# A graph network in four layers on one core: the projection of layer 0's second convolution in seven block products, with other buffers, fetches and start

## The chip, the cores and the metric

One core of one Trainium2 chip runs the whole program, in one launch. The metric is the device time in microseconds (us), the median of several runs. All arithmetic is fp32.

## The reference, cut to what matters

The input is 128 graphs of 64 nodes with 256 features, and one adjacency matrix of 64x64 for all. Four layers follow one another; each normalizes the features, takes the positive part, computes an update and adds it. The change is in layer 0, which is a graph convolution done twice and then four LSTMs over windows of 1, 2, 3 and 4 consecutive nodes, each of which writes its last hidden state back:

```python
h = jax.nn.relu(jnp.einsum('ts,bsh->bth', adj, x @ Wg0 + bg0))
h = jax.nn.relu(jnp.einsum('ts,bsh->bth', adj, h @ Wg1 + bg1))
for p in range(1, MAX_SKIP + 1):
    ...
    last = _lstm_last(Wih[p - 1], Whh[p - 1], bih[p - 1], bhh[p - 1], wins)
    h = h.at[:, idx, :].set(last.reshape(Bv, nw, Hd))
```

Here b is the graph and t the node. Layer 1 is a spectral convolution with attention and an MLP, layer 2 attention over a graph, layer 3 a transform with the eigenvectors of the graph's Laplacian; all of them use the same 64x64 matrix.

## The kernel before, in words

The 8192 tokens stand as 64 tiles of 128 tokens (two graphs each). Layer 0 works on 8 groups of 8 tiles (`NG`, `GT`), a group in two halves of 4 tiles (`HT`). Its results go to DRAM (`put`), and layers 1 to 3 work on 16 groups of 4 tiles, each of which runs through all three layers.

`layer0` (line 1411) does one group: fetch the tokens (two DMAs of 512 KB), norm statistics (`ln_stats`, line 1289: two DVE instructions a tile, four on POOL for the group of tiles), positive part on ACT, product with the adjacency (`mix`, line 1259, a burst of 64x64 matmuls), product with `Wg[0]`, a second mix into `ayT`, and then, feature-major, the projection with `Wg[1]` into `hT`. That projection makes, for each half and each of the two blocks of 128 output rows, two accumulated products of 128x128 by 128x512; its evacuation is a DVE maximum with the bias and a POOL addition. Then the LSTM steps follow: the first step of each window by `lstm_step` (line 1309), the later ones by `lstm_fast` (line 1359). `lstm_fast` computes a 2x2 block product in 7 block products instead of 8: sums of the weight blocks are made once (`fastw`, line 1165, on POOL), sums of the data blocks by `pieces` (line 1343), and partial results are passed on by ACT copies and DVE additions between two PSUM buffers, one of kind "bank" and one of kind "seed". At the end of a group the tokens are fetched a second time, to be added.

The order of all instructions is made ahead by `Plan` (lines 61 to 350): every operation is recorded with an engine and a cost, `schedule` (line 232) runs through the time of a model of the engines and puts the ready operation of the best rank next, and `issue` (line 343) emits them in that order. So every engine's queue has a fixed order, and in the profile every instruction has line 349; tiles tell them apart. What sets the order:

- `rank` (line 333): older groups first; a `lead` makes an operation count as of an older or younger group. The eigen-decomposition of the 64x64 matrix (`spectrum`, line 1193; group `EIG`) runs beside layer 0 on DVE with the lowest rank, on PE and POOL with the highest. Its work space, the arena, serves as big buffers once it is done.
- `window` (line 1052): how many groups may be under way; one more for fetches on SP.
- Pools of buffers (line 904): `big` (128x1024), `mid` (128x512), `stat`, `attn`, 6 PSUM banks and 2 seeds. A value takes a free buffer when its first operation is placed; `reserve` (line 1055) keeps some for the oldest group. After layer 0, `more(mids, ...)` (line 1050) turns the middle buffers into big ones.
- `plan.behind`: an operation that is recorded while it is set waits for the one it names.
- `burst` (line 105): what is recorded inside is one indivisible operation of the plan.

At the start (lines 1097 to 1160) ACT's queue fetches group 0's tokens in five pieces, SP's queue the weights; 14 products of a matrix of ones come first on PE; then row sums of the adjacency are made (`pb`, line 1146: one product with ones, one with the column `rscol`) and the bias tables C0T and B1T from them. Group 0 does its front two tiles at a time.

Of the kernel before, what the change touches and what calls it, by code (L numbers as in the profile page):

```python
# [8 lines left out]
ALU = mybir.AluOpType  # L9
# [3 lines left out]
N = 64  # L13
# [55 lines left out]
class Plan:  # L69
# [111 lines left out]
    def cost(op, aps):  # L181
# [7 lines left out]
        if op.name == "dma_start" and op.eng != "SP":  # L189
            return 0.6, 4.0  # L190
# [713 lines left out]
NBIG, NMID, NSTAT, NATTN = 14, 10, 14, 4  # L904
# [108 lines left out]
def gnn_kernel(ctx: ExitStack, tc: tile.TileContext, a, out):  # L1013
# [38 lines left out]
    def window(oldest):  # L1052
        return max(oldest, 0) + 3 - oldest if oldest < NG - 1 else REST + 4 - oldest if oldest < REST else 8
# [92 lines left out]
    pb = bank("rs")  # L1146
    PE.matmul(pb[:, :N], ones[:N], adjT2[:N], start=True, stop=True)
    PE.matmul(pb[:, N:2 * N], rscol[:N].to_broadcast([N, P]), adjT2[:N], start=True, stop=True)
    rsrow = C([P, 2, 2, N], "rsrow")
    V.tensor_copy(rsrow, pb[:, :2 * N].rearrange("p (r n) -> p r n", r=2).unsqueeze(2).to_broadcast([P, 2, 2, N]))  # L1150


    V.tensor_scalar(nB0, nB0, rscol, -1.0, op0=ALU.mult, op1=ALU.mult)
    C0T = C([P, 2, P], "C0T")
    B1T = C([P, 2, 2, P], "B1T")
    row = lambda r: rsrow[:, r].rearrange("p r n -> p (r n)")
    for c in range(2):
        V.tensor_scalar(C0T[:, c], row(1), bgc[0][:, c:c + 1], None, op0=ALU.mult)
        for t in range(2):
            V.tensor_scalar(B1T[:, t, c, :], row(0), bgc[1][:, c:c + 1], 1.0 if t else -1.0, op0=ALU.mult, op1=ALU.mult)  # L1160
# [128 lines left out]
    def ln_stats(src, n=HT):  # L1289
# [8 lines left out]
        G.tensor_scalar(rs[:, 0, :], mv[:, :, 1], 1e-5, None, op0=ALU.add)  # L1298
        G.tensor_tensor(rs[:, 0, :], rs[:, 0, :], mhalf[:, :n], op=ALU.pow)
        G.tensor_tensor(rs[:, 1, :], mv[:, :, 0], rs[:, 0, :], op=ALU.mult)  # L1300
        G.tensor_scalar(rs[:, 1, :], rs[:, 1, :], -1.0, None, op0=ALU.mult)
# [108 lines left out]

    def layer0(fetched):
        x = fetched()
        plan.lead = 1
# [3 lines left out]
        for t0 in range(0, GT, nl):  # L1417
# [7 lines left out]
            ps = mix(lambda t, c: h[t // 2][:, t % 2, tok(c)], lambda t: adjTb, nl)  # L1425
            for j in range(0, nl, 2):
# [17 lines left out]
        for hf in range(2):  # L1444
            ts = slice(hf * GT // 2, (hf + 1) * GT // 2)
            for m in range(2):
# [3 lines left out]
                dst = hT[m].rearrange("p (n t) -> p n t", t=GT)[:, :, ts]  # L1450
                b1 = [B1T[:, i, m, :].unsqueeze(2).to_broadcast([P, P, GT // 2]) for i in range(2)]
                V.tensor_tensor(dst, ps.rearrange("p (t n) -> p n t", n=P), b1[0], op=ALU.max)
                G.tensor_tensor(dst, dst, b1[1], op=ALU.add)
# [367 lines left out]
```

## Time and profile before

| | |
|---|---|
| time, median of 3 runs | 2100.99 us (2100.03 to 2101.82) |
| profiled execution: time, span | 2099.95 us, 2098.2 us |
| mean granted TensorE clock | 0.998 |
| PE, DVE, ACT, POOL busy | 2065.2, 1767.8, 1097.0, 777.8 us |
| layer 0's groups stored | from 232 us (group 0) to 1340 us (group 7) |
| first product of layer 1 | 1283.7 us |
| last write of the eigenvectors, their first use in layer 3 | 1227.8 us, 1473.4 us |

In the profile PE is TensorE's matmul, PEld its weight load, DVE VectorE, ACT ScalarE, POOL GpSimd, SP the queue that issues DMAs. A line of a group of instructions has the engine, the operation, what is written and read, the shapes and the count; then the busy time in us and the mean of one in ns; then the engine's idle time just before them. Each fp32 product shows as two matmul records. A line of a stretch has its ends, its length, and for each engine the busy time and, in brackets, the number of instructions; the last three numbers are the granted TensorE clock, the DMA engines' busy share and GB/s.

### The profile page before, as it was taken

How to read it: one execution, taken by the hardware profiler on the slowest of the kernel's cores; microseconds unless marked ns; L12 is line 12 of the kernel's file. 1: busy time of each engine (PE TensorE's matmuls, PEld its weight loads, DVE VectorE, ACT ScalarE, POOL GpSimd, SP SyncE). 2: the span in 40 equal slices, each digit the busy share in tenths (PEclk: the TensorE clock that was granted, in tenths of full speed). 3: DMA queues.
4: the chain of work that ended last, by engine and by line, in shares of the span. 5: the costliest groups of instructions: out<-in, count | busy, mean ns of one | idle time of the engine just before them, and what ended most of it. 6: DMA issues, size and time to landing. Idle time of an engine off the chain costs nothing.

```text
span 2098.2 us, 48166 instructions
## 1 busy us (share of the span) xinstructions
PE 2065.2 (98%) x17928; PEld 1678.8 (80%) x17928; DVE 1767.8 (84%) x6691; ACT 1097.0 (52%) x2465; POOL 777.8 (37%) x1162
## 2 busy tenths in 40 slices
PE   8999999999999999999999999999999999999998
PEld 6689689689779778878878789987887788788776
DVE  7799899899999999999988954877878878885787
ACT  3344544544443453444444435575667666664674
POOL 7422221221211122022010123677557576854354
PEclk9999999999999999999999999999999999999999
DMA  6000100100100100000000211200100100000001
GB/s 231 1 3 3 63 2 2 62 2 2 61 1 1 61 2 1 21 26 2 30 12 1 98 44 33 82 2 1 42 22 1 35 29 22 12 12 11 2 1 62
DMA packets 44875, 57.84 MB, mean 28 GB/s; under 512 B 8928, under 2 KB 38496, under 8 KB 44640
## 3 DMA queue, kind: packets, MB, share of 16 engines
q1 hardware_dynamic: 43536, 53.71, 8.0%
q8 instruction: 141, 2.31, 0.5%
q10 hardware_dynamic: 1104, 1.05, 0.2%
q14 instruction: 94, 0.77, 0.1%
HBM read 37.53 MB, written 16.78 MB: 26 GB/s over the span
## 4 chain that ended last, share of the span: by engine, by line
PE 87%; DVE 10%; issue 1%; ACT 1%; POOL 0%; DMA 0%; DVEq 0%; ACTq 0%
PE bank L349 70%; PE seed L349 17%; DVE big L349 3%; DVE arena L349 3%; DVE stat L349 2%; DVE mids L349 1%; ACT mids L349 1%; DVE sums L349 1%; DMA big<-in_x_dram 0%; DVE seed L349 0%; POOL stat L349 0%; DVE Whh L349 0%; ACT big L349 0%; DVE bank L349 0%; DMA adjT<-in_adjT_dram 0%
## 5 line engine op out<-in xcount | busy, mean ns | idle before, releaser
L349 PE MATMUL bank<-big,Wih 128*128 128x512 f32 (+4 forms) x1800 | 552.1, 425 | 1.1 <-DVE big L349 0.7
L349 PEld LDWEIGHTS bank<-big,Wih 128*128 128x128 f32 x1800 | 315.4, 190 | 141.6 <-issue 95.9
L349 PE MATMUL bank<-big,sums 128*128 128x128 f32 (+3 forms) x1936 | 361.5, 301 | 5.8 <-DVE big L349 2.5
L349 ACT ACTIVATE mids<-bank,bl 128x512 f32<-128x512 f32 (+2 forms) x432 | 246.8, 576 | 206.3 <-PE bank L349 191.9
L349 PE MATMUL bank<-big,Whh 128*128 128x128 f32 (+3 forms) x1304 | 322.5, 333 | 1.4 <-ACT big L349 1.4
L349 PEld LDWEIGHTS bank<-big,sums 128*128 128x128 f32 (+1 forms) x1936 | 286.5, 188 | 40.8 <-issue 17.7
L349 DVE TENSOR_TENSOR arena<-arena 64x42 f32<-64x42 f32 (+6 forms) x1358 | 275.0, 230 | 18.6 <-POOL arena L349 0.3
L349 PEld LDWEIGHTS bank<-big,Whh 128*128 128x128 f32 x1304 | 215.3, 191 | 22.6 <-issue 10.7
L349 ACT ACTIVATE mids<-seed,bl 128x256 f32<-128x256 f32 (+2 forms) x192 | 102.1, 532 | 225.4 <-PE seed L349 223.2
L349 DVE TENSOR_TENSOR big<-mids 128x512 f32<-128x512 f32 (+2 forms) x256 | 154.7, 613 | 27.3 <-ACT mids L349 24.9
L349 POOL TENSOR_SCALAR stat<-stat 128x4 f32<-128x4 f32 (+1 forms) x236 | 70.7, 300 | 260.7 <-DVE stat L349 247.9
L349 PE MATMUL seed<-big,sums 128*128 128x128 f32 (+3 forms) x800 | 141.0, 299 | 0.0
L349 DVE SCALAR_TENSOR_TENSOR arena<-arena 64x1 f32<-64x1 f32 (+16 forms) x565 | 128.7, 251 | 10.6 <-ACT arena L349 3.5
L349 POOL TENSOR_TENSOR big<-big,B1T 128x512 f32<-128x512 f32 x32 | 37.8, 1186 | 255.1 <-DVE big L349 233.8
L349 ACT COPY seed<-bank 128x128 f32<-128x128 f32 (+2 forms) x192 | 53.8, 280 | 145.7 <-PE bank L349 143.8
L349 ACT ACTIVATE mids<-big 128x256 f32<-128x256 f32 (+2 forms) x176 | 89.4, 510 | 74.2 <-DVE big L349 71.5
L349 POOL TENSOR_TENSOR stat<-stat,mhalf 128x4 f32<-128x4 f32 (+1 forms) x118 | 126.2, 1069 | 5.2
L349 ACT COPY mids<-bank 128x256 f32<-128x256 f32 (+3 forms) x320 | 107.6, 357 | 38.7 <-PE bank L349 36.8
L349 POOL MEMSET arena<- 64x2 f32 (+5 forms) x72 | 7.8, 113 | 306.2 <-DVE arena L349 301.7
L349 PEld LDWEIGHTS seed<-big,sums 128*128 128x128 f32 (+1 forms) x800 | 115.8, 189 | 3.5 <-issue 0.3
L349 DVE TENSOR_SCALAR arena<-arena 64x1 f32<-64x1 f32 (+8 forms) x506 | 102.3, 211 | 6.8 <-POOL arena L349 0.3
L349 PE MATMUL seed<-big,Whh 128*128 128x128 f32 (+3 forms) x424 | 103.6, 326 | 0.3 <-DVE big L349 0.3
(507 smaller groups left out, 4615.9 us busy)
## 6 DMA issues: line engine op xcount, KB each, us to landing
big<-in_x_dram SPq DMA_DIRECT2D x29, 512.0 KB, 5.2
put<-big SPq DMA_DIRECT2D x15, 512.0 KB, 3.0
big<-put SPq DMA_DIRECT2D x9, 512.0 KB, 6.4
out_dram<-big SPq DMA_DIRECT2D x18, 256.0 KB, 2.3
Wih<-in_WihT_dram SPq DMA_DIRECT2D x3, 1024.0 KB, 12.0
Whh<-in_WhhT_dram SPq DMA_DIRECT2D x3, 1024.0 KB, 13.6
sums<-put SPq DMA_DIRECT2D x5, 512.0 KB, 4.1
out_dram<-sums SPq DMA_DIRECT2D x10, 256.0 KB, 2.2
```

Of the source, the lines that this page charges most:

```text
L349: getattr(self.engines[op.eng], name)(*map(real, args), **{k: real(a) for k, a in kw.items()})
```

## The change

1. The projection with `Wg[1]` is done by `proj_seed` for groups 1 to 7: 7 products of 128x128 by 128x256 for each half, with sums of the weight blocks made once (`fastg`, four POOL subtractions and additions of 128x128) and sums of the data blocks by `pieces` on POOL. Group 0 keeps the old form. The evacuation is the same.
2. The sums take 512 columns; `NMID` goes from 10 to 9.
3. `window` lets four groups of layer 0 be under way where it let three.
4. The first fetch of a group waits for the last PE operation of the projection of the group before (`gone`).
5. At the start: 16 more products of ones, recorded for group 0 with a lead of -5, so that the plan places them where PE has nothing else ready; the row sums and the bias tables (`rows`) are recorded inside group 0, behind its first mix; the four POOL operations of a norm form one burst in group 0; the plan's cost of a DMA on ACT's queue becomes 0.5 us to issue and 1.6 us plus its size over 100 GB/s to land (it was 0.6 and 4.0 us whatever the size).

```diff
-            return 0.6, 4.0
+            return 0.5, 1.6 + free(aps[0]) * aps[0].ap[0][1] * 4e-6 / 0.1
...
-NBIG, NMID, NSTAT, NATTN = 14, 10, 14, 4
+NBIG, NMID, NSTAT, NATTN = 14, 9, 14, 4
...
-        return max(oldest, 0) + 3 - oldest if oldest < NG - 1 else REST + 4 - oldest if oldest < REST else 8
+        return max(oldest, 0) + 4 - oldest if oldest < NG - 1 else REST + 4 - oldest if oldest < REST else 8
...
+    plan.group, plan.lead = 0, -5
+    for i in range(16):
+        PE.matmul(warm[:, P:2 * P], ones, ones, start=True, stop=True)
+    plan.group, plan.lead = SETUP, 0
...
+    a11, a12, a21, a22 = (Wg[1][:, k, m * P:(m + 1) * P] for m in range(2) for k in range(2))
+    s1, s2, s3, s4 = (C([P, P], f"fastg{j}") for j in range(4))
+    G.tensor_tensor(s1, a21, a22, op=ALU.add)
+    G.tensor_tensor(s2, s1, a11, op=ALU.subtract)
+    G.tensor_tensor(s3, a11, a21, op=ALU.subtract)
+    G.tensor_tensor(s4, a12, s2, op=ALU.subtract)
+    fastg = {1: a11, 2: a12, 3: s4, 4: a22, 5: s1, 6: s2, 7: s3}
...
+    def proj_seed(L, R, out):
+        w = HT * P // 2
+        r, d = bank("hT"), plan.value("seed")
+        m1, m5, c11, c12 = r[:, :w], r[:, w:2 * w], d[:, :w], d[:, w:2 * w]
...
+        with plan.burst(2 * (0.001672 * w + 0.006)):
+            prod(m5, 5, True)
+            prod(m1, 1, True)
+        u = mid()[:, :w]
+        ACT.copy(c11, m1)
+        ACT.copy(u, m5)
+        prod(m1, 6)
+        prod(c11, 2)
+        V.tensor_tensor(c12, m1, u, op=ALU.add)
+        prod(m1, 7)
+        prod(c12, 3)
+        V.tensor_tensor(m5, m1, u, op=ALU.add)
+        prod(m1, 4)
+        out(0, d)
+        out(1, r)
...
+        plan.behind = gone.get(plan.group - 1)
         x = fetched()
+        plan.behind = None
...
+            if plan.group == 0 and t0 == 0:
+                plan.behind = plan.ops[-1]
+                rows()
+                plan.behind = None
...
+            if plan.group:
+                proj_seed(fastg, pieces(lambda c, n: ayT[hf][:, c, n * HT * P // 2:(n + 1) * HT * P // 2], G), out)
+                continue
             for m in range(2):
                 ps = bank("hT")
                 for c in range(2):
                     PE.matmul(ps, Wg[1][:, c, tok(m)], ayT[hf][:, c, :], start=c == 0, stop=c == 1)
...
+                out(m, ps)
+        gone[plan.group] = [op for op in plan.ops[-40:] if op.eng == "PE"][-1]
```

`prod(ps, i)` is one product of the weight sum i with the data sum i, accumulated onto what stands in `ps` unless told to start. `rows` holds the lines of `pb`, `rsrow`, C0T and B1T of the kernel before, unchanged.

More of the change, by code (lines that the diff above doesn't have):

```diff
@@ L1 @@
-from contextlib import ExitStack, contextmanager
+from contextlib import ExitStack, contextmanager, nullcontext
 import concourse.bass as bass
@@ L1145, in gnn_kernel, with rows @@
     V.reduce_sum(rscol, adj2, axis=AX.X)
-    pb = bank("rs")
-    PE.matmul(pb[:, :N], ones[:N], adjT2[:N], start=True, stop=True)
-    PE.matmul(pb[:, N:2 * N], rscol[:N].to_broadcast([N, P]), adjT2[:N], start=True, stop=True)
     rsrow = C([P, 2, 2, N], "rsrow")
-    V.tensor_copy(rsrow, pb[:, :2 * N].rearrange("p (r n) -> p r n", r=2).unsqueeze(2).to_broadcast([P, 2, 2, N]))
-    V.tensor_scalar(nB0, nB0, rscol, -1.0, op0=ALU.mult, op1=ALU.mult)
     C0T = C([P, 2, P], "C0T")
     B1T = C([P, 2, 2, P], "B1T")
[L1156 to L1160, printed above, removed]
+    def rows():
+        pb = bank("rs")
+        PE.matmul(pb[:, :N], ones[:N], adjT2[:N], start=True, stop=True)
+        PE.matmul(pb[:, N:2 * N], rscol[:N].to_broadcast([N, P]), adjT2[:N], start=True, stop=True)
+        V.tensor_copy(rsrow, pb[:, :2 * N].rearrange("p (r n) -> p r n", r=2).unsqueeze(2).to_broadcast([P, 2, 2, N]))
+        row = lambda r: rsrow[:, r].rearrange("p r n -> p (r n)")
+        for c in range(2):
+            V.tensor_scalar(C0T[:, c], row(1), bgc[0][:, c:c + 1], None, op0=ALU.mult)
+            for t in range(2):
+                V.tensor_scalar(B1T[:, t, c, :], row(0), bgc[1][:, c:c + 1], 1.0 if t else -1.0, op0=ALU.mult, op1=ALU.mult)
+    V.tensor_scalar(nB0, nB0, rscol, -1.0, op0=ALU.mult, op1=ALU.mult)
     G.tensor_tensor(bl, bl, bh, op=ALU.add)
@@ L1297, in ln_stats @@
             V.bn_aggr(mv[:, t, :], st[:, t, :])
[L1298 to L1301, printed above, removed]
+        with plan.burst(1.04 + 0.14 * n) if plan.group == 0 else nullcontext():
+            G.tensor_scalar(rs[:, 0, :], mv[:, :, 1], 1e-5, None, op0=ALU.add)
+            G.tensor_tensor(rs[:, 0, :], rs[:, 0, :], mhalf[:, :n], op=ALU.pow)
+            G.tensor_tensor(rs[:, 1, :], mv[:, :, 0], rs[:, 0, :], op=ALU.mult)
+            G.tensor_scalar(rs[:, 1, :], rs[:, 1, :], -1.0, None, op0=ALU.mult)
         return lambda t: rs[:, 0, t:t + 1], lambda t: rs[:, 1, t:t + 1]
@@ L1409, in lstm_fast, with prod @@
             V.tensor_mul(dst, o, th)
+    def proj_seed(L, R, out):
+        w = HT * P // 2
+        r, d = bank("hT"), plan.value("seed")
+        m1, m5, c11, c12 = r[:, :w], r[:, w:2 * w], d[:, :w], d[:, w:2 * w]
+        def prod(ps, i, start=False):
+            PE.matmul(ps, L[i], R[i], start=start, stop=True, skip_group_check=True)
+        with plan.burst(2 * (0.001672 * w + 0.006)):
[13 more added lines that the diff above has]
+        out(1, r)
+    gone = {}
     def layer0(fetched):
+        plan.behind = gone.get(plan.group - 1)
         x = fetched()
+        plan.behind = None
         plan.lead = 1
@@ L1445, in layer0, with out @@
             ts = slice(hf * GT // 2, (hf + 1) * GT // 2)
+            def out(m, ps):
+                dst = hT[m].rearrange("p (n t) -> p n t", t=GT)[:, :, ts]
+                b1 = [B1T[:, i, m, :].unsqueeze(2).to_broadcast([P, P, GT // 2]) for i in range(2)]
+                V.tensor_tensor(dst, ps.rearrange("p (t n) -> p n t", n=P), b1[0], op=ALU.max)
+                G.tensor_tensor(dst, dst, b1[1], op=ALU.add)
+            if plan.group:
+                proj_seed(fastg, pieces(lambda c, n: ayT[hf][:, c, n * HT * P // 2:(n + 1) * HT * P // 2], G), out)
+                continue
             for m in range(2):
@@ L1449, in layer0 @@
                     PE.matmul(ps, Wg[1][:, c, tok(m)], ayT[hf][:, c, :], start=c == 0, stop=c == 1)
[L1450 to L1453, printed above, removed]
+                out(m, ps)
+        gone[plan.group] = [op for op in plan.ops[-40:] if op.eng == "PE"][-1]
         plan.lead = 0
```

## The prediction

> **What bounds the kernel now.** I read the page first: the busy shares, the 40 slices and the chain that ended last.
>
> ```profile
> span 2098.2 us, 48166 instructions
> PE 2065.2 (98%) x17928; PEld 1678.8 (80%) x17928; DVE 1767.8 (84%) x6691; ACT 1097.0 (52%) x2465; POOL 777.8 (37%) x1162
> ...
> PE   8999999999999999999999999999999999999998
> ...
> DVE  7799899899999999999988954877878878885787
> ...
> PE 87%; DVE 10%; issue 1%; ACT 1%; POOL 0%; DMA 0%; DVEq 0%; ACTq 0%
> ```
>
> TensorE is busy in every slice and holds 87% of the last chain. Only 33.0 us of the span have no matmul in flight, so no change of waiting alone can bring much more than that; the sure gain is fewer streamed columns. DVE stands at 9 tenths as long as layer 0 lasts (to about 1340 us): it is the next to run out.
>
> Second view: the groups of matmuls by form.
>
> ```profile
> L349 PE MATMUL bank<-Wg,mids 128*128 128x256 f32 x256 | 67.8, 394 | 0.0
> L349 PE MATMUL bank<-big,Wg 128*128 128x512 f32 x128 | 61.7, 598 | 0.0
> ...
> L349 PE MATMUL seed<-big,sums 128*128 128x256 f32 x128 | 33.2, 379 | 0.0
> ```
>
> The middle row is the projection that is changed: 64 products of 512 columns (8 groups, 2 halves, 2 rows, 2 blocks) show as 128 records, two passes for each fp32 product. The last row is a part of the 256-column products that the LSTM steps already do in sevens. A mean includes the pipeline's tail, so I price by the distance between starts of neighbouring records: median 429 ns for a 512-column pass (775 pairs) and 216 ns for a 256-column pass (3217 pairs). A product costs 0.858 us or 0.432 us.
>
> Third view: stretches of the span, the start first.
>
> ```profile
> 0.00:37.50 37.50, 32.10 (x354) 23.92 (x354) 25.32 (x110) 8.52 (x20) 26.15 (x49) 0.91 0.94 321
> ...
> 1342.00:2098.20 756.20, 739.85 (x8418) 597.68 (x8416) 603.04 (x1757) 490.63 (x932) 465.87 (x634) 1.00 0.07 21
> ```
>
> ```profile
> 8.00:10.00 2.00, 0.88 (x34) 0.82 (x34) 1.93 (x11) 0.97 (x2) 1.25 (x4) 1.00 0.74 161
> 10.00:12.00 2.00, 1.31 (x45) 0.99 (x37) 2.00 (x13) 1.78 (x5) 1.76 (x6) 0.58 1.01 202
> 12.00:14.00 2.00, 2.00 (x10) 1.73 (x7) 1.23 (x13) 1.14 (x3) 0.86 (x4) 0.50 1.01 377
> ```
>
> Before 37.5 us TensorE idles for 5.4 us, and after the sparse matmuls of 7 to 10 us its granted clock falls to 0.50, from 10.3 to 17.2 us. Layers 1 to 3 alone (from 1342 us) leave 16.4 us idle, layer 0 with its hand-over (37.5 to 1342 us) some 11.
>
> **What the skill says.** "TensorE: Matmul & The Clock Gate", section "Back-to-back issue gap", gives N/2.4 + 2.5 ns for a warm pass; with two passes per column that is 215.8 ns for 256 columns: the trace's 216. Its "Part 1: The HAM clock gate" says that a window of 3.4 us with too little work halves the clock; the trace shows that at 10.3 us. "SBUF — State Buffer", section "SBUF: two separate sides": a DVE instruction with two SBUF inputs and a GpSimd instruction exclude each other for their whole length. The trace agrees: a 64x64 scalar_tensor_tensor, of about 0.25 us, takes 3.68 us at 24.83 us, while POOL runs 1.26 us additions without a gap.
>
> **The change, part by part.**
>
> *Seven products for eight.* In 7 of 8 groups each half now runs 7 products of 256 columns in place of 4 of 512: 7 x 0.432 = 3.02 us for 4 x 0.858 = 3.43 us, 0.41 us less. Fourteen halves: **-5.7 us**, on the engine that sets the end.
>
> What it adds lies on other engines. ACT: two copies of 128x256 a half (0.36 and 0.39 us), 14 x 0.75 = 10.4 us, hidden at 45% load. DVE: two additions from PSUM of 128x256 (0.427 and 0.426 us), 14 x 0.85 = 11.9 us. POOL: four subtractions of 0.77 to 0.78 us, 14 x 3.1 = 43 us, and four of 128x128 once (about 0.55 us each), at some 20% load. DVE has about 95 us idle between 100 and 1200 us, and more than half of its layer 0 work is the eigen-decomposition (writes and reads of the arena, 635 of 1052 us between 37.5 and 1197 us), which yields to all else. So the 12 us, and some waiting behind POOL's 43, push back the eigen-decomposition: it ends at 1228 us, perhaps 20 to 40 us later afterwards. Its result is first multiplied at 1473 us, so that costs nothing itself; but its arena becomes four big buffers for the later layers, where a delay can open gaps. Cost 0 to 4 us, taken with the buffers below.
>
> The seven products hang on copies and additions (copy 0.36 + copy 0.39 + two additions of 0.43 = 1.6 us a half). Other groups' products cover that; without cover it would be 14 x 1.6 = 22 us.
>
> *Nine middle buffers.* The weight sums (512 columns) take the place of one. An LSTM step of the oldest group can hold 8 (four gates, two each); of the rest, other groups keep at most one where they had two. And after layer 0 the middle buffers serve as big ones: 4608 columns give 4 of 1024, not 5, so 34 in place of 35. No view shows how full the pools are. The skill's "Perfetto Trace Analysis", section "Optimization Strategy", reads repeating bubbles as a sign of too few buffers; the trace's bubbles are small (16.4 us in 756 us). From below: 0. From above: 1/35 of the concurrency behind 756 us at 2.2% idle; if idle time grew by a third, +5 us. I take **+1.0 us** with the arena's delay.
>
> *Four groups under way, tokens fetched later.* The fourth group gives PE more to choose from; the upper bound of that gain is the 11 us idle in layer 0, of which most is the fixed start and stop of small bursts. The fetch of a group now waits for the last product of the group before. For group 3 on this changes little: its fetch is already at 210 to 234 us, just after group 2's projection (191 to 213). For group 1 it moves from 14 us to after 37 us: landing 5.2, statistics of four tiles about 2.2, POOL 1.7, ACT 2.1 give a first mix at 48.4 us instead of 46.4; group 0's first LSTM step holds 24 products x 0.858 = 20.6 us from 37.6 on and covers that. On SP's queue the stores of finished groups and their second fetch stand behind the waiting fetch; these have tens of us to spare. Taken at **0**, from -5 to +3.
>
> *The start.* Sixteen filler products of 128 columns (two passes of 112 ns each: 3.6 us at full rate) keep PE at work from 7.2 to about 10.7 us. If the clock stays up, the 12 passes of 256 columns that now run at half rate save 12 x 0.215 = 2.6 us; but the first mix, at 9.48 us now, starts up to 1.2 us later behind the fillers. The row sums' products leave PE's queue ahead of that mix, where they now wait until 9.12 us for the column sums, and POOL's four steps of a norm stay together; both only help what the fillers delay anyway. Sum **-1.5 us**, from -4 (the eigen-decomposition's 1.8 us wait at 26 us goes too) to +1.5 (the fillers delay, and the clock falls all the same).
>
> Sum: -5.7 + 1.0 + 0 - 1.5 = -6.2 us. The profiled execution took 2099.95 us (1.75 us around its span), which gives 2093.8; the median of the runs is 1.0 above that execution, which gives 2094.8. I say **2094**.
>
> **The rivals.**
>
> *Slower: steps starve for middle buffers.* Layer 0 has 88 LSTM steps (11 a group). At the end of a step the chain gate (ACT, 0.68 us) to state (DVE, 0.70 us) is 1.4 us long, covered by other groups' front work, whose tokens, mixed tokens and outputs need middle buffers too. If in one step of eight nothing is ready, 11 x 1.4 = 15 us come in: 2109. It decides from 0.07 us a step (5.7/88), where the saved products are gone. For it speaks that each half of a front holds four at once; against it that PE's waits name mids with 3.3 us in all, and that the late fetch frees big buffers instead.
>
> *No change: the saving is given back.* DVE, at 93 to 95% from 700 to 1000 us, gets 12 us more and POOL's lock; 4 to 6 us of new waits, in the hand-over to layer 1 above all, leave about 2099. For it: DVE is the next bound. Against it: more than half of DVE's load yields.
>
> *More: the fourth group pays.* Half of layer 0's idle time goes, another -5: 2089, or less if the start gives its whole -4. For it: idle stretches do lie there. Against it: they are pieces below 1 us.
>
> That the change saves no columns is excluded: it counts them.
>
> **How the numbers follow.** Chances: forecast 0.58 (own range 2090 to 2097), more 0.14, no change 0.12, slower 0.16. One run of this kernel differs from another by up to 1.8 us; I count 0.2%, 4.2 us, as the least that can be told from no change. Faster 0.72, same 0.12, slower 0.16. Range 2085 to 2104: below lies the best end of "more", above most of the slower case.
>
> **What would show it.** Right: projection rows of 128x256 from groups 1 to 7, 98 products (196 records) beside 8 products of 512; PE's busy time down by about 6 us with idle at 33 or less; a clock of 1.00 from 7 us on; eigen-decomposition ending after 1228 us without effect. Wrong: PE idle in layer 0 above 15 us, with waits for DVE or ACT on mids; idle after 1342 us well above 16.4; a hole between 37 and 60 us where group 1's tokens come late; a clock of 0.5 in spite of the fillers.

## The result, and the profile after

The changed kernel takes 2105.11 us (median of 22 runs, 2101.84 to 2106.56), the kernel before, run beside it, 2101.52 us (22 runs, 2098.51 to 2103.30): a ratio of 1.0017, 95% interval 1.0010 to 1.0023. So it is about 3.6 us slower, where 7 us faster was forecast, and just above the range's end of 2104. The profiled execution took 2104.42 us, with a span of 2102.6 us.

The page of the changed kernel: span, busy times (share of the span), the slices of PE and DVE, the chain that ended last.

```profile
span 2102.6 us, 48557 instructions
PE 2065.6 (98%) x18044; PEld 1695.1 (81%) x18044; DVE 1791.8 (85%) x6719; ACT 1106.1 (53%) x2493; POOL 815.2 (39%) x1222
...
PE   8999999999999999999999999999999999999998
...
DVE  7789999889899999999998985877878878895787
...
PE 84%; DVE 13%; issue 1%; ACT 1%; POOL 1%; DVEq 0%; ACTq 0%
```

PE's share of the last chain fell from 87 to 84%, DVE's rose from 10 to 13%: PE waits more for DVE. PE has 37.0 us of the span without a matmul, where it had 33.0. Its busy time did not fall, but that is no sign that the saving is missing: it now holds the fillers (3.7 us). Another 2 to 3 us of busy time are not accounted for; time at half rate is not it, for the span has 8.0 us of that where it had 9.1. The groups of matmuls by form show the projection of groups 1 to 7:

```profile
L349 PE MATMUL bank<-big,fastg 128*128 128x256 f32 x84 | 25.1, 380 | 0.0
```

The 84 records here and 28 into a seed are the four products with a weight sum (4 x 2 passes x 14 halves); with 84 for the three that use Wg as it stands, that is the 196 that were forecast. Adding up the records of both traces, each at the usual distance between starts for its size (429 ns for 512 columns, 216 for 256, and so on), gives 5.7 us less of streamed work after than before, fillers left out: as worked out.

Where it went is seen with the stretches, of the changed kernel first, then of the kernel before.

```profile
0.00:37.50 37.50, 34.55 (x394) 25.93 (x394) 26.37 (x107) 8.27 (x20) 29.30 (x53) 1.00 0.84 295
37.50:234.00 196.50, 191.75 (x1523) 156.04 (x1524) 167.52 (x762) 90.90 (x252) 77.65 (x129) 0.99 0.05 13
...
1197.00:1342.00 145.00, 139.10 (x1113) 123.72 (x1112) 105.94 (x377) 67.03 (x160) 52.91 (x82) 1.00 0.18 55
1342.00:2102.60 760.60, 743.49 (x8428) 599.72 (x8426) 610.31 (x1760) 492.69 (x935) 466.12 (x635) 1.00 0.07 22
```

```profile
37.50:234.00 196.50, 195.03 (x1532) 155.41 (x1533) 172.43 (x821) 88.19 (x250) 66.94 (x113) 1.00 0.04 10
...
1197.00:1342.00 145.00, 140.79 (x1111) 124.69 (x1111) 87.49 (x252) 69.99 (x166) 49.77 (x78) 1.00 0.20 61
```

Between 37.5 and 234 us PE idles for 4.75 us where it idled for 1.47; in the hand-over from 1197 to 1342 us for 5.9, where it was 4.2. Busy time alone misses what half rate and the order do, so I used a second measure: the streamed work that starts after a given moment, in both traces, each record at its usual distance between starts. Below this is called the work that remains; its difference says which kernel is ahead. By it the changed kernel is ahead by 8.4 us at 37 us (the 5.7 saved, and 2.7 won at the start), by 5.3 at 45, by 2.9 at 200, by 1.1 at 1200; at 1342 it is 2.2 behind, at 2050 3.0 behind. So three places took the gain: 5.5 us between 37 and 200 us, 3.3 us in the hand-over, and a slow drift.

The waits of PE (engine and tiles, what it waited for: us in total, times, longest) name the first, for the changed kernel and then for the kernel before.

```profile
PE bank L349 <- DVE arena L349: 11.1, 18, 1.8
PE bank L349 <- DVE big L349: 5.6, 7, 1.7
```

```profile
PE bank L349 <- DVE arena L349: 5.8, 8, 1.8
PE bank L349 <- DVE big L349: 4.1, 7, 1.2
```

The arena is the eigen-decomposition's work space, which the forecast took to yield to everything. The time line of the changed kernel near 37 us (start, length, engine, and in brackets the idle time before and its releaser) shows how it does not.

```profile
35.41 1.10 POOL L349 TENSOR_TENSOR big<-big,B1T 128x512 f32<-128x512 f32 x1
...
35.73 3.37 DVE L349 SCALAR_TENSOR_TENSOR arena<-arena 64x1 f32<-64x1 f32 x2
...
36.48 1.26 POOL L349 TENSOR_TENSOR sums<-Wih,sums 128x512 f32<-128x512 f32 x1
37.70 1.25 POOL L349 TENSOR_TENSOR sums<-Whh 128x512 f32<-128x512 f32 x1
...
39.16 0.38 PE L349 MATMUL bank<-arena,ones 128*128 128x1 f32 x2 [1.84 <-DVE arena L349]
...
39.41 8.81 PE L349 MATMUL bank<-big,Wih 128*128 128x512 f32 x16
```

POOL runs additions of 128x512 for the LSTM's weight sums without a gap until 38.95 us. DVE's two small instructions, some 0.3 us of work (one like them takes 0.14 us at 39.04), end at 39.10. The tiny matmul that needs their result has the highest rank on PE, so it stands ahead of the LSTM products of group 0 in PE's queue, and those wait though their data are there (the addition that the next ones read ended at 36.51). Then the granted clock falls: the 16 records of 512 columns take 8.81 us, 551 ns each.

The kernel before has the same hold, earlier, and PE stops just as long behind it, 1.84 us, with products ready behind the tiny matmul there too:

```profile
24.83 3.68 DVE L349 SCALAR_TENSOR_TENSOR arena<-arena 64x64 f32<-64x64 f32 x1
...
28.57 0.38 PE L349 MATMUL bank<-arena,ones 128*128 128x1 f32 x2 [1.84 <-DVE arena L349]
28.82 1.96 PE L349 MATMUL bank<-big,Wg 128*128 128x512 f32 x4
```

So the stop itself is no loss against the kernel before; it only comes later, and 1.8 of the 2.7 us of lead at 37 us are there because it has not come yet. What is new is the half rate after it. In these traces the stretches between two changes of the granted clock are multiples of 3.41 us long (34.13, 6.83, 3.41), so each trace can be laid on a grid of that step. The whole stop of the changed kernel falls into one step of its grid, and the stop of the kernel before is parted between two, with 0.67 and 1.17 us. The steps around the stop, of the changed kernel first; the fall of the clock follows in its second line:

```profile
36.36:39.77 3.41, 1.57 (x6) 0.65 (x5) 2.98 (x5) 0.00 (x0) 2.59 (x3) 1.00 0.00 0
39.77:43.18 3.41, 3.41 (x5) 1.33 (x4) 3.38 (x17) 0.28 (x1) 3.03 (x4) 0.50 0.00 0
```

```profile
23.99:27.40 3.41, 2.74 (x41) 1.81 (x40) 3.18 (x2) 0.00 (x0) 3.41 (x4) 1.00 1.02 405
27.40:30.82 3.42, 2.25 (x11) 1.01 (x15) 2.73 (x10) 0.00 (x0) 1.59 (x2) 1.00 1.07 364
30.82:34.23 3.41, 3.41 (x41) 1.91 (x41) 2.62 (x7) 0.00 (x0) 2.44 (x3) 1.00 1.10 348
```

Of the 5.5 us lost between 37 and 200 us, 3.1 fall before 45 us (the stop and the half rate) and 2.4 after it, where DVE instructions are held behind POOL's sums again (three of 1.3 to 1.8 us between 46 and 52 us) and PE waits another 1.25 us at 51.6.

### The profile page after: what moved, and what is told of

Read it like the earlier page. It is cut to its first block, busy times and chain, and to the rows that moved or that the text cites. A ratio compares the mean times of both kernels' runs of the same rounds, so it can differ in the third digit from the quotient of the medians.

```text
span 2102.6 us, 48557 instructions
## 1 busy us (share of the span) xinstructions
PE 2065.6 (98%) x18044; PEld 1695.1 (81%) x18044; DVE 1791.8 (85%) x6719; ACT 1106.1 (53%) x2493; POOL 815.2 (39%) x1222
## 4 chain that ended last, share of the span: by engine, by line
PE 84%; DVE 13%; issue 1%; ACT 1%; POOL 1%; DVEq 0%; ACTq 0%
PE bank L349 67%; PE seed L349 17%; DVE arena L349 5%; DVE big L349 4%; DVE stat L349 2%; DVE mids L349 1%; ACT mids L349 1%; POOL stat L349 0%; DVE sums L349 0%; DVE seed L349 0%; DVE bank L349 0%; DVE Whh L349 0%; ACT big L349 0%; POOL arena L349 0%; POOL sums L349 0%
## 5 line engine op out<-in xcount | busy, mean ns | idle before, releaser
L349 PE MATMUL bank<-big,Whh 128*128 128x128 f32 (+3 forms) x1260 | 302.7, 326 | 0.4 <-ACT sums L349 0.4
L349 DVE TENSOR_TENSOR arena<-arena 64x42 f32<-64x42 f32 (+6 forms) x1361 | 282.9, 235 | 18.3 <-POOL arena L349 0.8
L349 PEld LDWEIGHTS bank<-big,Whh 128*128 128x128 f32 x1260 | 207.7, 191 | 17.1 <-issue 8.0
L349 POOL TENSOR_TENSOR big<-big 128x256 f32<-128x256 f32 (+2 forms) x76 | 52.6, 694 | 373.5 <-DVE big L349 230.3
L349 DVE TENSOR_TENSOR big<-mids 128x512 f32<-128x512 f32 (+2 forms) x256 | 149.8, 594 | 23.7 <-ACT mids L349 21.4
L349 DVE SCALAR_TENSOR_TENSOR arena<-arena 64x1 f32<-64x1 f32 (+17 forms) x565 | 130.6, 257 | 5.8 <-POOL arena L349 2.2
L349 ACT COPY seed<-bank 128x128 f32<-128x128 f32 (+2 forms) x206 | 58.9, 286 | 145.4 <-PE bank L349 131.0
L349 ACT ACTIVATE mids<-big 128x512 f32<-128x512 f32 (+2 forms) x176 | 88.9, 509 | 67.2 <-DVE big L349 61.2
L349 POOL TENSOR_TENSOR big<-big,big 128x128 f32<-128x128 f32 (+2 forms) x168 | 100.6, 616 | 14.7 <-DVE arena L349 7.8
L349 DVE TENSOR_TENSOR big<-big,mids 128x256 f32<-128x256 f32 (+2 forms) x198 | 100.4, 513 | 6.9 <-ACT mids L349 6.2
```

What stands on the lines that cost most here:

```text
L349: getattr(self.engines[op.eng], name)(*map(real, args), **{k: real(a) for k, a in kw.items()})
```

## The experiments

All are compared with the kernel before on the same chip, whose median there lay between 2100.15 and 2101.71 us; differences to the changed kernel are to its 2105.11 us, and uncertain by 1 to 2 us each. In e1 to e5, e9 and e11 the order of instructions is that of the kernel edited, so an edit changes one cost and not the plan. In e6 the order differs in layers 1 to 3; the others get a new plan.

**e1: without the fillers.**

```diff
-    for i in range(16):
+    for i in range(0):
         PE.matmul(warm[:, P:2 * P], ones, ones, start=True, stop=True)
```

> The changed kernel without its 16 filler products; the plan gives every other instruction the same place. If the fillers are worth what they were made for (the clock at the start), the clock falls to 0.5 at about 10 us again, group 0's first LSTM product starts 2 to 3 us later than 34.3 us, and the time is 2 to 3 us above the changed kernel's (about 2107.5). If what they gain is taken back by 60 us anyway, as the changed kernel's waits between 36 and 60 us suggest, the time is the changed kernel's within 1 us (2104 to 2106). If they only stand in the way of the first mix, it is 1 us below.

2101.76 us, ratio 1.0001 (0.9993 to 1.0009): 3.3 us faster than with them, more than any of the three cases had. The fillers cost time. Where, the trace does not show: the profiled execution, at 2104.35, is the slowest of its thirteen. But it shows two things that bear on the argument. The clock does not fall at 10 us in this execution (in those of e7 and e9, also without fillers, it does, for 3.41 us), and the hold is there without the fillers:

```profile
34.45 3.85 DVE L349 SCALAR_TENSOR_TENSOR arena<-arena 64x1 f32<-64x1 f32 x2
38.36 0.38 PE L349 MATMUL bank<-arena,ones 128*128 128x1 f32 x2 [2.32 <-DVE arena L349]
38.60 8.81 PE L349 MATMUL bank<-big,Wih 128*128 128x512 f32 x16
```

Group 0's first LSTM product starts 1.3 us earlier here (32.97 us for 34.30), and PE then stops even longer, with half rate after it.

**e2: the last of the seven products done twice.** The result of the projection is another one; the plan places the pair as one product.

```diff
+        plan.tag = 'twice'
         prod(m1, 4)
+        plan.tag = None
```

> The changed kernel, same order, with the last product of each seven done twice (so the projection's result is another one): 14 more products of 256 columns, 14 x 0.432 = 6.0 us of TensorE. If a column is worth its full time there, 6 us above the changed kernel (2111): then the saved products did pay, and the loss lies elsewhere. If TensorE has slack at these places because the seven products wait for copies and additions, less than 2 us above (below 2107): then the saving was never there to be had.

2108.44 us, ratio 1.0035 (1.0023 to 1.0048): 3.3 us more for 14 x 0.432 = 6.0 us of products. This lies between the two theories: by the medians a streamed column is worth some 55% of its time here. The interval is wide: it reaches from 4.8 to 10.1 us above the kernel before, where the changed kernel stands at 3.6, so the 6.0 us may cost anything from 1.2 us to their full time. In the profiled executions only 1.0 us of them is taken from PE's stops (37.0 us without a matmul in the changed kernel, 36.1 here); another 1.3 us is less time at half rate, near the end of the kernel and far from the edit. So a column is worth at least a part of its time; how large a part stays open.

**e3: ACT's copies and DVE's additions of the projection on 16 of 256 columns, its four POOL subtractions a half as memsets.** The projection's result is another one. A tag set while an operation is recorded tells `issue` what to emit in its place, and the plan still reckons with the operation itself.

```diff
+                    if op.tag == 'thin' and op.eng == 'G':
+                        self.engines['G'].memset(real(args[0]), 0.0)
+                        continue
+                    if op.tag == 'thin':
+                        args = [real(a) for a in args]
+                        args = [a[:, :16] if len(a.shape) == 2 else a[:, :, :16] for a in args]
```

> The changed kernel, same order, with the work beside the seven products thinned: POOL's four subtractions a half become memsets, the two copies on ACT and the two additions on DVE do 16 of 256 columns (so the projection's result is another one). Takes about 10 us from DVE, 9 from ACT and 25 from POOL in layer 0. If that side work ate the saving, 4 us or more below the changed kernel (2101 or less). If the start and the hand-over to layer 1 ate it, within 1.5 us of it (2103.6 to 2105).

2102.06 us, ratio 1.0005 (0.9997 to 1.0013): 3.0 us less, between the two cases. The side work is not free.

**e11: only the POOL subtractions as memsets** (result another one, as in e3).

```diff
-                proj_seed(fastg, pieces(lambda c, n: ayT[hf][:, c, n * HT * P // 2:(n + 1) * HT * P // 2], G), out)
+                plan.tag = 'thin'
+                R = pieces(lambda c, n: ayT[hf][:, c, n * HT * P // 2:(n + 1) * HT * P // 2], G)
+                plan.tag = None
+                proj_seed(fastg, R, out)
```

> The changed kernel, same order, with the four POOL subtractions of each half as memsets (so the projection's result is another one); the copies on ACT and additions on DVE stay. The third experiment, which thinned all of them, gained 3.0 us. If POOL's subtractions cost it by keeping DVE out, 2 to 3 us below the changed kernel (2102 to 2103). If DVE's additions did, within 1 us of the changed kernel's 2105.1.

2102.51 us, ratio 1.0006 (0.9997 to 1.0014): 2.6 us less. That is nearly all of e3's 3.0, so it is POOL's four subtractions, not the copies or DVE's additions, that cost. By the work that remains the gain comes in layer 0 (2.2 us at 1342 us). And it comes by way of DVE: with the same instructions in the same order DVE is busy for 1027.8 us between 52 and 1197 us, in the changed kernel for 1037.6. PE hardly waits for the differences themselves: its waits that end with POOL sum to 0.4 us in the changed kernel.

**e4: POOL's sums of the weights (fastw and fastg) as memsets of the same tiles.** The sums are zero, so the results of the LSTM steps and of the projection are other ones.

```diff
     fastw = {}
+    plan.tag = 'thin'
     for p in (1, 2, 3):
...
     fastg = {1: a11, 2: a12, 3: s4, 4: a22, 5: s1, 6: s2, 7: s3}
+    plan.tag = None
```

> The changed kernel, same order, with POOL's sums of the weight blocks (28 instructions, some 33 us between 14 and 52 us) replaced by memsets, which read nothing (so the LSTM steps and the projection compute with zeros in those sums). If the loss between 36 and 60 us comes from DVE instructions of the eigen-decomposition that stand behind POOL's additions while a matmul that waits for them holds TensorE's queue, the 1.84 us wait at 39 us and the half clock after it go, and the time falls by 3 to 5 us (2100 to 2102). If the wait has another cause, it stays and the time is within 1 us.

2097.15 us, ratio 0.9980 (0.9972 to 0.9988): 8.0 us less, more than the 3 to 5 that were expected. The time line of this kernel at the same place:

```profile
34.61 0.98 POOL L352 MEMSET sums<- 128x512 f32 x2
...
35.31 0.28 PE L357 MATMUL bank<-arena,ones 128*128 128x1 f32 x2
...
35.45 7.11 PE L357 MATMUL bank<-big,Wih 128*128 128x512 f32 x16
```

The tiny matmul has no idle time before it, and the 16 records after it take 7.11 us, 444 ns each. The stretch from 37.5 to 45 us, first of the changed kernel, then of this one:

```profile
37.50:45.00 7.50, 5.84 (x11) 2.61 (x12) 5.22 (x22) 2.09 (x3) 6.15 (x10) 0.77 0.00 0
```

```profile
37.50:45.00 7.50, 7.50 (x23) 3.71 (x22) 5.54 (x26) 6.66 (x11) 6.47 (x13) 1.00 0.00 0
```

PE is never idle and the clock stays at 1.00. By the work that remains, e4 is 1.8 us ahead of the changed kernel at 37 us, 5.6 at 45, 7.3 at 100 and 7.9 at 200. The memsets also take less of POOL's time (0.49 us in place of 1.26), so e4 alone does not part the lock from POOL's lateness; DVE's 3.37 us for 0.3 us of work, and PE's wait that ends with DVE, speak for the lock.

**e5: the same memsets in the kernel before**, which has fastw alone.

```diff
     fastw = {}
+    plan.tag = 'thin'
     for p in (1, 2, 3):
```

> The kernel before, same order, with POOL's sums of the weight blocks replaced by memsets (the LSTM steps compute with zeros in those sums): what the fourth experiment did to the changed kernel, which gained 8.0 us. If POOL's additions at the start cost both kernels alike, it gains 7 to 8 us as well (about 2094), and they explain nothing of the difference. If it is the changed order that runs into them, it gains 3 to 5 us (2096.5 to 2098.5), and 3 to 5 us of the lost gain lie there. The difference of the two kernels without these additions is then what the rest of the change is worth.

2099.25 us, ratio 0.9988 (0.9981 to 0.9994): only 2.5 us less. The weight sums cost the changed kernel 8.0 - 2.5 = 5.5 us more than the old one. Without them the changed kernel would be 2.1 us the faster of the two. By the work that remains e5 gains 2.1 us up to 37 us, where the old stop lay, and only 1.0 us from there to 200 us, where e4 gains 6.1.

**e9: no fillers and the sums as memsets** (the results differ as in e4).

```diff
-    for i in range(16):
+    for i in range(0):
...
+    plan.tag = 'thin'
     for p in (1, 2, 3):
```

> The changed kernel, same order, without the fillers and with POOL's weight sums as memsets: the first and the fourth experiment together (the LSTM steps and the projection compute with zeros in the sums). If the fillers' 3.3 us are a cost of their own, 3 us below the fourth experiment's 2097.2 (about 2094). If they only cost because the front they push back then meets POOL's additions, the two losses are one, and the time is the fourth experiment's within 1 us.

2096.09 us, ratio 0.9971 (0.9960 to 0.9982): 1.1 us below e4, not 3.3. So by the medians most of what the fillers cost is the same loss as that of the sums. How the two meet is not shown: e1's trace has the hold and the stop without fillers.

**e6: the 35th big buffer.** fastg lies in the room behind nine middle buffers, which is free for the later layers as a big one.

```diff
-    mids = C([P, NMID * 512], "mids")
+    mids = C([P, (NMID + 1) * 512], "mids")
...
-    s1, s2, s3, s4 = (C([P, P], f"fastg{j}") for j in range(4))
+    s1, s2, s3, s4 = (mids[:, NMID * 512 + j * P:NMID * 512 + (j + 1) * P] for j in range(4))
```

> The changed kernel with the weight sums of the projection in the room behind the nine middle buffers, so that after layer 0 these 5120 columns make five big buffers again, 35 in all; the plan is the same up to about 1600 us. If the missing buffer costs layers 1 to 3 time, 2 to 2.5 us below the changed kernel (2102.8). If layers 1 to 3 have buffers enough, within 1 us of it.

2101.95 us, ratio 1.0000 (0.9991 to 1.0008): 3.2 us less. The order of layers 1 to 3 is another one with the buffer. The trace shows 1.1 us of the gain up to 2050 us, all after 1600 us. e13 below, which also has 34 big buffers where the kernel before has 35, loses nothing in layers 1 to 3 (18.3 us behind at 1342 us, 18.2 at 2050). So the 3.2 us are the buffer's price in this plan, and no general one.

**e7: e6, without fillers, and eight of the sums (`p` = 1, the windows of two nodes) on DVE in place of POOL.**

```diff
+            E = V if p in (1,) else G
-            G.tensor_tensor(s1, a21, a22, op=ALU.add)
+            E.tensor_tensor(s1, a21, a22, op=ALU.add)
```

> The changed kernel with the 35th buffer, without fillers, and with the eight weight sums of the two-node window, the first of POOL's block, on DVE. If POOL's block of additions is what holds DVE at the start, its first third leaves, and the time is 3 us below that of the run without fillers less what the buffer gives (about 2097). If DVE is itself the bound in layer 0, its 5.4 us more put the eigen-decomposition back and the time stays at 2101 or more.

2096.75 us, ratio 0.9975 (0.9965 to 0.9984). This kernel does all the work. By the work that remains it is ahead of the kernel before by 10.5 us at 37 us, 5.7 from the products and 4.8 from the start, though its clock stood at half rate for 18.1 us of the whole execution (11.1 in the kernel before). So neither the fillers nor the clock of the first microseconds were needed for the start's gain.

**e8: e7 with nine big buffers reserved for the oldest group in place of eight.** This changes nothing but the order.

```diff
-            return {"big": 8, "mid": 5, "stat": 1, "attn": 0, "bank": 2, "seed": 1}[kind]
+            return {"big": 9, "mid": 5, "stat": 1, "attn": 0, "bank": 2, "seed": 1}[kind]
```

> As the seventh, with one big buffer more kept for the oldest group of layer 0 (9 in place of 8), which the plan orders differently from the first group on. If the difference between kernels is a matter of such orders as much as of work, it differs from the seventh by 2 us or more, either way; if the work decides, by less than 1 us.

2100.80 us, ratio 0.9994 (0.9987 to 1.0001): some 4 us more than e7, from order alone. Between 800 and 900 us e8 falls from 3.8 us ahead of the kernel before to 1.7 behind, by the work that remains; e13 below has its hole there too.

**e10: the products and nine middle buffers alone, with the old window, fetch and start.** What is undone, against the changed kernel; the plan's cost of a DMA and the burst of POOL's norm operations go back too:

```diff
-        return max(oldest, 0) + 4 - oldest if oldest < NG - 1 else REST + 4 - oldest if oldest < REST else 8
+        return max(oldest, 0) + 3 - oldest if oldest < NG - 1 else REST + 4 - oldest if oldest < REST else 8
...
-    for i in range(16):
+    for i in range(0):
...
+    rows()
     V.tensor_scalar(nB0, nB0, rscol, -1.0, op0=ALU.mult, op1=ALU.mult)
...
-        plan.behind = gone.get(plan.group - 1)
         x = fetched()
-        plan.behind = None
```

> The seven products and the nine middle buffers alone: three groups under way, tokens fetched as before, the start as before. If the products pay by themselves and the rest of the change loses it, 2 to 4 us below the kernel before (2098 to 2100). If they do not pay for their side work and the buffer, as fast as before or slower (2101.5 or more).

2109.47 us, ratio 1.0036 (1.0023 to 1.0048): 8 us slower than before, with the saved columns in it. Up to 400 us it keeps the 5.7 us of lead, at 700 it has none, at 1000 it is 6.4 behind. Its start is as before, and so is the stop of 1.84 us, at 26.7 to 28.6 us: so it is the edits of the start or of the fetch that move it, for e14 below, with the old window, has it moved too.

**e13: the kernel before with nine middle buffers and nothing else.**

```diff
-NBIG, NMID, NSTAT, NATTN = 14, 10, 14, 4
+NBIG, NMID, NSTAT, NATTN = 14, 9, 14, 4
```

> The kernel before with nine middle buffers instead of ten, and nothing else (34 big buffers after layer 0). The tenth experiment was 8.0 us slower than before with the seven products and nine buffers. If the buffer is what costs (the rival of steps that starve), 8 us or more slower than before (2109 or more), with TensorE idle in layer 0 between the LSTM steps. If the seven products cost it, within 4 us of before (2105 or less), of which 3 are the 35th big buffer's.

2120.91 us, ratio 1.0103 (1.0088 to 1.0118): 20.8 us slower. The trace is level with the kernel before until about 800 us; then one place takes 18 to 20 us, some 12 of them without a matmul and some 7 by half rate. The stretches of e13, and then of the kernel before:

```profile
800.00:850.00 50.00, 43.41 (x337) 38.77 (x336) 45.96 (x181) 20.08 (x52) 5.32 (x12) 0.96 0.07 22
850.00:900.00 50.00, 44.33 (x397) 38.38 (x397) 45.10 (x174) 13.55 (x39) 2.98 (x4) 0.90 0.08 28
```

```profile
800.00:850.00 50.00, 49.54 (x365) 43.06 (x362) 46.21 (x171) 19.10 (x50) 11.11 (x14) 1.00 0.01 2
850.00:900.00 50.00, 50.00 (x295) 37.09 (x294) 47.21 (x171) 22.84 (x54) 6.21 (x9) 1.00 0.14 48
```

In the middle of it, in e13's time line:

```profile
865.02 3.07 DVE L349 TENSOR_REDUCE arena<-arena 64x21 f32<-64x1344 f32 x1
865.82 0.28 PE L349 MATMUL bank<-big,sums 128*128 128x128 f32 x1
...
869.14 0.80 PE L349 MATMUL bank<-big,sums 128*128 128x128 f32 x2 [3.05 <-DVE big L349]
```

Here an LSTM chain over ACT and DVE stands behind a reduction of the eigen-decomposition on DVE, 3.07 us long, and PE waits 3.05 us for it. There is no shortage in every step: groups 0 to 4 are stored within 1.3 us of their times in the kernel before (up to 892 us); the hole is in the work beside and after them.

**e14: the changed kernel with three groups under way.**

```diff
-        return max(oldest, 0) + 4 - oldest if oldest < NG - 1 else ...
+        return max(oldest, 0) + 3 - oldest if oldest < NG - 1 else ...
```

> The changed kernel with three groups of layer 0 under way instead of four, all else as it is. If the fourth group is what makes good for the missing middle buffer, 5 us or more slower than the changed kernel (2110 or more). If it only moves the last groups' fronts ahead and so empties the hand-over, as the twelfth experiment suggests, 2 to 4 us faster (2101 to 2103).

2121.81 us, ratio 1.0102 (1.0085 to 1.0119): 16.7 us slower than with four. But the mechanism is not that of layer 0: at 1200 us it is 3.4 us behind the changed kernel, at 1342 2.0, and at 2000 14.3. The loss lies in layers 1 to 3, which have the same work and the same buffers, in another order. 5.8 us of it are PE without a matmul between 1342 and 2000 us (13.2 for 7.4); the rest is not traced.

**e12: e7, with three groups under way from the sixth on.**

```diff
-        return max(oldest, 0) + 4 - oldest if oldest < NG - 1 else ...
+        return max(oldest, 0) + (4 if oldest < 5 else 3) - oldest if oldest < NG - 1 else ...
```

> As the seventh experiment (2096.8), with three groups under way instead of four from group 5 on. With four, group 7's projection is done at 991 us, before the change at 1042: if the hand-over to layer 1 suffers because the last group's front is used up too early, the idle time of TensorE between 1197 and 1342 us (5.9 us in the changed kernel, 4.2 before) falls back to about 4 and the time is 1 to 3 us below the seventh. If the hand-over waits for the arena or for buffers, it stays within 1 us.

2092.49 us, ratio 0.9955 (0.9942 to 0.9967): the best here, 9 us below the kernel before, 4.3 below e7. The hand-over of e7, then of e12:

```profile
1197.00:1342.00 145.00, 140.96 (x1129) 128.83 (x1130) 102.47 (x367) 67.41 (x164) 49.59 (x77) 0.99 0.17 47
```

```profile
1197.00:1342.00 145.00, 141.23 (x1141) 128.79 (x1140) 105.84 (x377) 70.30 (x170) 54.52 (x83) 1.00 0.19 56
```

The gain is larger than expected and comes another way. While group 5 is the oldest, groups 5 to 7 are under way with three as with four; what the edit holds back is the work after layer 0. PE idles for 4.0 us there in e7 already, for 3.8 in e12. Group 7's projection runs from 970 to 1000 us in both, for PE's order is the same up to 1202 us; that the last group's front is used up too early is not borne out by this pair. The two plans part at 1185 us, when DVE begins with norm statistics in e7 and goes on with the eigen-decomposition in e12. What follows on PE, in e7 and then in e12:

```profile
1193.96 0.59 PE L349 MATMUL bank<-big,sums 128*128 128x256 f32 x2
1197.48 0.70 PE L349 MATMUL bank<-big,sums 128*128 128x256 f32 x2 [2.92 <-DVE big L349]
```

```profile
1194.29 1.04 PE L349 MATMUL bank<-big,sums 128*128 128x256 f32 x4
1195.17 0.59 PE L349 MATMUL bank<-big,Wih 128*128 128x256 f32 x2
```

One stop of 2.92 us behind DVE, with half rate from 1198.2 to 1201.6 us after it (some 1.7 us lost), is there in e7 and not in e12. Together that is the whole 4.3 us.

**e15: the products with ten middle buffers, and no room taken for their sums** (two lie in `rsrow` and one in `same`, which is filled later, one in place of `a21`), the rest as before. **e16: the same, with six big buffers reserved in layers 1 to 3 in place of seven.** They were to show what the products bring alone.

```diff
+        s1, s2 = (rsrow[:, r].rearrange("p r n -> p (r n)") for r in range(2))
+        G.tensor_tensor(s1, a21, a22, op=ALU.add)
+        G.tensor_tensor(s2, s1, a11, op=ALU.subtract)
+        G.tensor_tensor(same, a12, s2, op=ALU.subtract)
+        G.tensor_tensor(a21, a11, a21, op=ALU.subtract)
```

e16 adds to this:

```diff
-        return {"big": 7, "mid": 0, "stat": 2, "attn": 1, "bank": 2, "seed": 0}[kind]
+        return {"big": 6, "mid": 0, "stat": 2, "attn": 1, "bank": 2, "seed": 0}[kind]
```

> The seven products with all ten middle buffers (their weight sums made after group 0's projection in room that is free during layer 0: two in the row sums' table, one in place, one in a table that layer 2 fills later); three groups under way, fetches and start as before. If the saved columns are worth their time once no buffer is lost, layer 0's last store is at 1333 to 1335 us (1340 before): 5.7 us and no more. If the side work takes them, at 1339 or later. Layers 1 to 3 get another order from the plan by this, so the whole time says less: 2096 to 2110.

> As the fifteenth, with 6 big buffers kept for the oldest group of layers 1 to 3 in place of 7, which orders only these layers anew: layer 0's last store is where the fifteenth has it (within 1.5 us), and the whole time differs by 5 us or more if the order of layers 1 to 3 decides; if the saved work decides, both are 4 to 6 us below the kernel before (2095 to 2097).

2124.89 us, ratio 1.0109 (1.0095 to 1.0123), and 2116.93 us, ratio 1.0075 (1.0061 to 1.0089). Layer 0's last store is at 1349 us in both, 8 us later than before, with all ten buffers. By the work that remains, e15 is 3.2 us ahead of the kernel before at 200 us and 7.3 behind at 900: a hole between 800 and 900 us again. From 1342 to 2000 us it falls back by 12 more. The 8 us between e15 and e16 are the order of the later layers alone. So what the products would bring in an undisturbed order stays open. The start of both has a stop of 3.3 us, to 28 us, behind a DVE instruction of 4.74 us, and half rate after it.

## Why the prediction was wrong, step by step

**Seven products for eight, -5.7: the work is right, its value is not shown.** The trace has the 196 records and 5.7 us less of streamed work. By e2's median such a column is worth about 55%, some 3.1 us, but e2's interval also allows the full value. The forecast took PE's 98% for a queue that does not stop for others. It read the 11 us of idle time in layer 0 as mostly the start and stop of small bursts; the trace of the kernel before says otherwise, for 10.6 of the 11.2 us are waits that another engine ended, DVE in most of them.

**"Cost 0" of the side work.** The copies and DVE's additions did cost next to nothing (e3 against e11: 0.4 us, within the error). POOL's 43 us, set at nothing for its load of 20%, cost 2.6 us (e11). A low load hides no lock: by the Trainium skill's "SBUF — State Buffer", section "SBUF: two separate sides", which the forecast cited, a POOL instruction that reads SBUF and a DVE instruction with two inputs there exclude each other. e11 agrees: without POOL's reads DVE is busy 9.8 us less with the same instructions. That this is what makes PE 2.6 us later is argued, not shown.

**The start, -1.5: this step failed.** The forecast had it that PE would win clock and lose a little behind the fillers, and that at best the wait at 26 us would go. Up to 37 us PE won 2.7 us, more than I took, but the wait did not go. It moved to 37.3 us, just as long (1.84 us), and this time half rate followed it, from 39.8 to 43.2 us; at 45 us the lead was 5.3 us, less than the 5.7 saved. Later holds behind the same sums took 2.4 us more up to 200 us. POOL's weight sums, which the forecast did not price beyond four small new ones, cost the changed kernel 5.5 us more than the kernel before (e4 against e5). I had the evidence in hand: the 3.68 us at 24.83 us. I used it as an example of the lock and priced DVE's whole load, but did not ask where the same hold would fall once the steps before it had moved, nor whether the clock would fall with it. Which edit moved it is open: not the fillers alone, since e1 has it too. The clock at the start, 2.6 us in the sum, was worth little: e7 has no fillers and the larger gain. The Trainium skill's "TensorE: Matmul & The Clock Gate", section "Part 1: The HAM clock gate", says that the window runs free and that the slow start differs from run to run. The traces agree: full rate begins at 6.92 us before, at 5.6 after, at 4.07 to 6.99 in other profiled executions. So where a stop falls on the grid is luck in part, and another execution of either kernel may have it otherwise; no second trace of one kernel is there to tell.

**Nine middle buffers, +1.0: wrong in size.** The 35th big buffer is worth 3.2 us in this plan (e6), near the upper end of the 0 to 5 that I gave. e13 shows the other half: with nine middle buffers the old kernel loses 20.8 us. The rival "steps starve for middle buffers" thus had its cause, but not its mechanism: not 1.4 us in one step of eight, but one hole of 18 to 20 us between 800 and 900 us. In the changed kernel that hole is not there (PE idles for 1.3 us between 731 and 889 us); four groups under way and the other edits give another order.

**Four groups, late fetch, 0.** The fetch does not wait at all on the chip: `plan.behind` only sets a place in the order. Group 1's first fetch is issued at 13.7 us, not after 37, and 9 of the first token fetches run before 30 us where 10 did. The window's price depends on the order that comes with it: three groups cost 16.7 us in one plan (e14, by way of layers 1 to 3), and three at the end gained 4.3 us in another (e12, by one stop that is not there). "More: the fourth group pays" is not borne out as it was told: PE idles for 17.0 us between 37.5 and 1342 us, where it did for 11.2. That is one of the forecast's own signs of being wrong (above 15 us in layer 0); most of the waits end with DVE's work on `arena` and `big`, though; those that end on `mids` sum to 0.9 us in the whole span.

**The eigen-decomposition** ends at 1268 us, 40 us later, as foreseen, and its result is needed far later. Its instructions cost by standing ahead of others on PE and DVE. Whether its later end costs too is not settled: in the hand-over, where 3.3 us are lost, DVE now spends 39 us on the arena between 1197 and 1342 us, where it spent 14, and PE's longest wait there (1.71 us, at 1208.6) ends with DVE. No experiment parts this from the order.

**The sum.** By the medians: products -3.1, weight sums +5.5, the 35th buffer +3.2, POOL's subtractions +2.6, the start -2.7 make +5.5, against +3.6 measured. The terms overlap (e9; and part of the start's 2.7 is the stop that comes later) and each comparison has 1 to 2 us of uncertainty, so I claim the terms' signs and order of size, not the remainder; that the total comes near is luck in part. What I did wrong beyond single terms is to price an edit to a planned order as a sum of work. Any edit reorders all that comes after: order alone moved the time by 4 us (e8), by some 8 (e15 against e16) and by 14 us in layers that the edit does not touch (e14). A range from 9 us below the forecast to 10 us above it had little room for that.

## What to carry to other kernels

When an edit moves a step, look up what that step collides with now, and where the same collision will fall at its new place: a stop that costs the same at both may bring half rate at one and not at the other. Where a planner orders a kernel, separate an edit from the order that comes with it: keep the order and change one cost (e2, e4, e11), and keep the work and change the order (e8), before either is given the credit. When two plans differ, find the first instruction at which they part: e12's gain lay in one stop there, and not where I had looked for it. And do not take an engine at 98% at its full time without a test: double a piece of its work once, and run it often enough for the interval to decide.

## What was not expected of the hardware

- A DVE instruction can be held over several POOL instructions in a row, not only the one that runs: 3.37 us and 3.68 us for some 0.3 and 0.25 us of work, over additions of 1.26 us.
- One stop of PE of 1.84 us was enough for half rate, and the same stop elsewhere was not. Half rate followed in all seven traces that have the stop between 36 and 40 us, where it falls whole into one step of 3.41 us of the clock's grid (the changed kernel, e1, e2, e3, e6, e11, e14; 2.1 us of a stop of 2.32 in e1). It followed in none of the three that have it between 26 and 29 us, where it is parted between two steps (the kernel before, e10, e13).
- Adding up all 18 traces by such steps at full rate: of those with 1.92 us or more without a matmul, half rate followed all 21; with 1.45 to 1.92 us, 20 of 39; with less, 3 of 10,916, all within the first 11 us.
